# Low-rank adapter and paged attention on one core: another order of the first loads, of the first step's products, and of one weight read

## The chip, the cores and the metric

The kernel runs on one core of a Trainium2 chip. The metric is the device time of one execution in microseconds (us), the median of the runs shown. The core has a matrix engine (PE, with its weight load PEld), a vector engine (DVE), a scalar engine (ACT), GpSimd (POOL) and SyncE (SP), which here only issues DMAs. Each engine works through its own instructions in the order of the program. SP and ACT issue DMAs on hardware queues (q1 and q10 in the profile), POOL on a software queue (q0).

## The reference, cut to what matters

```
x: (8, 128, 512) f32
# 1. an adapter for each batch element
x = x + einsum('bsi,boi->bso', x, L0_weight[itok_B])          # L0_weight: (16, 512, 512)
# 2. paged attention, 32 query heads, 8 key heads, D = 128
q, k, v = x @ Wq.T, x @ Wk.T, x @ Wv.T
q, k = rope(rmsnorm(q) * wq_norm, pos), rope(rmsnorm(k) * wk_norm, pos)
                                                  # pos = seqlens[b] + 0..127
K = concat(k_cache[block_table[b]], k)            # 512 cached keys and 128 new ones
V = concat(v_cache[block_table[b]], v)            # cached keys from seqlens[b] on are masked
p = softmax(q @ K.T / sqrt(128) + mask)           # 4 query heads share a key head
out = x + (p @ V) @ Wo.T
```

All tensors are float32. The block table, the lengths and the adapter numbers are inputs that the kernel reads at run time.

## The kernel before, in words

**Steps.** The heads are cut into 4 groups `g` of 2 key heads and 8 query heads. A step is a pair (group, batch element): `i = 8 * g + b`, 32 steps in all. Step `i` computes the scores of its 8 query heads, one at a time (`h` = 0 to 7: a product on PE into `sc`, L977; the masked negative minimum on DVE, L987; the exponential on ACT, L1003; the normalisation on POOL, L1051; a transposition on DVE, L819). A place `8 * i + h` is called a slot.

**What PE does between the scores.** A list `main` holds the other products of a step in pieces of one fourth each: the projections of the next step (`project(i + 1, ...)`: `kv` for keys and values, `q0` and `q1` for four query heads each), the values product of the step before (`values`), its output product (`output`), and in the first group the adapter product (`lora_y`). The pieces are spread over the 8 heads by a share of the estimated cost (UNIT for a piece, TR for one 128x128 transposition). `turns_at` lists transpositions on PE at fixed heads: `turn_x`, `turn_x1` (x before and after the adapter), `turn_lora`, `turn_weights`, `turn_q`, `turn_k`.

**Products in flight.** Results of PE go to 4 PSUM tiles (`ps_mm`), shared by the transpositions and the products, and to 2 score tiles (`ps_sc`). What reads a product is not written down at once: `group` puts it into the list `pending`, and `run(pending)` writes it into the engines' queues later, once in each head after the scores, and at places of the prologue.

**After a projection.** `rotate` squares and sums the heads on ACT (L595), multiplies by the tables `CW` and `SW` on DVE (L607, L611) and adds the two on POOL (L620, L627); `norm_scales` makes the inverse root on POOL (L634, L635); its `rest` scales q on ACT (L640) and k on DVE (L643). `turn_q` and `turn_k` then transpose q and k on PE (L720, L711) and copy them out of PSUM (L721, L712); the scores of the step need them.

**The prologue** (L874 to L932) prepares step 0. It loads x of element 0, the adapter `raw_lora`, the rows of Wk and Wv (`raw_kv`) and of Wq (`raw_q`); transposes them on PE, with copies on ACT; computes the row numbers of the paged gathers from the block table `bt_i` (`row_numbers`: one cast on DVE at L334 and a chain of 14 small operations on POOL, L336 to L342; `row_tables` writes `key_ix` and `val_ix` on DVE, L348 and L349); computes the sine and cosine tables from `len_i` and `ivf` (`rope_angles` with 10 operations on DVE, then Sin and Abs on ACT; `rope_cos`; `rope_table` on DVE); gathers K and V of element 0 with indirect DMAs on POOL (L559); and makes the adapter products of the elements 0 and 1 (`lora_y`, added to `acc` on DVE at L533). The projection `q1` of step 0 is not in the prologue; it is the first in `main` of step 0.

**The order of the loads.** SP issues `raw_lora`, Wk, the 4 tiles of Wq for `q0`, x of element 1, the adapter 1, Wq for `q1`, x of element 2 and 8 tiles of Wo; ACT issues x of element 0, `len_i`, `ivf`, Wv, `ids_i` and `bt_i`; POOL issues the two norm weights (`wn`). `len_i`, `ivf`, `ids_i`, `bt_i` and `wn` are small and are broadcast to all 128 partitions. The plain loads of SP and ACT take their semaphores from one set of eight, so that an issue waits until the load that had the semaphore before has landed.

**Later weights.** From group 1 on the weights go through DRAM: `send_weights` writes them block-transposed, and `receive_weights` reads them back on ACT's queue (L473) at the slots of `reads_at`. The 8 tiles of Wo for group `g` are read at

```python
read_at(8 * (B * g + 1) + n - n // 4 * 2, key)
```

that is at heads 0 to 3 for the first half (`o0`, n = 0 to 3) and at heads 2 to 5 for the second (`o1`, n = 4 to 7) of the group's second step, whose output product needs them near its end.

Of the kernel before, what the change touches and what calls it, by code (L numbers as in the profile page):

```python
# [11 lines left out]
FP = mybir.dt.float32  # L12
I32 = mybir.dt.int32
# [5 lines left out]
P = 128  # L19
# [33 lines left out]
def lora_then_paged_attention(  # L53
# [50 lines left out]
    def load_x(b, eng=None):  # L104
        (eng or nc.sync).dma_start(out=acc[b], in_=x[b])

    load_x(0, nc.scalar)
    len_i = const.tile([P, B], I32, name="len_i")
    nc.scalar.dma_start(out=len_i, in_=seqlens.partition_broadcast(P))
    ivf = const.tile([P, H2], FP, name="ivf")  # L110
    nc.scalar.dma_start(out=ivf, in_=inv_freq.partition_broadcast(P))


    def weight_rows(kind, g, n, m=1):
# [22 lines left out]
    def load_first(kind, n, m, eng):  # L137
        eng.dma_start(
            out=first[kind][:, n * 512 : (n + m) * 512].rearrange("p (n i) -> p n i", n=m),
            in_=weight_rows(kind, 0, n, m).rearrange("(n p) i -> p n i", p=P),  # L140
        )
        for k in range(n, n + m):
            raw[kind, 0, k] = first[kind][:, k * 512 : (k + 1) * 512]
# [2 lines left out]

    lraw = {}

    def load_lora(b, dst):
# [8 lines left out]
        nc.sync.dma_start(  # L158
            out=dst.rearrange("p (j i) -> p j i", j=4),
            in_=lora_w[bass.ds(n, 1), :, :].rearrange("m (p j) i -> p (m j) i", j=4),  # L160
        )

    def lora_tile(b):
        t = lora.tile([P, 4, REP, QK], FP, tag="raw", name=f"lraw_{b}")
        return t.rearrange("p a r k -> p (a r k)")[:, 0 : 4 * HID]

    load_lora(0, first["lora"])
    load_first("kv", 0, 2, nc.sync)
    load_first("kv", 2, 2, nc.scalar)
    load_first("q0", 0, 4, nc.sync)  # L170
    load_x(1)
    load_lora(1, lora_tile(1))
    load_first("q1", 0, 4, nc.sync)
# [17 lines left out]
    ident = const.tile([P, P], FP, name="ident")  # L191
    make_identity(nc, ident)
    inner = const.tile([P, 1], FP, name="inner")
    quad = const.tile([P, 1], FP, name="quad")
    for a in range(4):
# [21 lines left out]
    for m in masks:  # L217
        nc.gpsimd.memset(m[:, :, LC, :], 0.0)

    nc.gpsimd.dma_start(out=wn[:, 1, :], in_=k_norm_w.partition_broadcast(P))  # L220
    nc.gpsimd.dma_start(out=wn[:, 0, :], in_=q_norm_w.partition_broadcast(P))
# [51 lines left out]
    def read_at(slot, key):  # L273
        reads_at.setdefault(slot, []).append(key)

    for g in range(1, G):
        before = 8 * B * (g - 1)
        for k, kind in enumerate(("kv", "q0", "q1")):
            for n in range(4):
                turn_when[before + 9 + 5 * (4 * k + n) // 2] = len(turns_of)  # L280
                turns_of.append((kind, g, n))
                read_at(before + 8 * (B - 2) + (2, 4, 6)[k] + n, (kind, g, n))
        for n, slot in enumerate((39, 42, 45, 62, 64, 66, 68, 70)):
            key = (f"o{n // 4}", g, n % 4)
# [155 lines left out]

    def turn_weights(key, copy=nc.scalar.copy):
        kind, a, n = key
        if n == 0:
            wT[kind] = wts.tile([P, 4, 4, 4, Q4], FP, tag=kind, name=f"w_{kind}_{a}")
        t = ps_mm.tile([P, HID], FP, tag="mm", name="wt_{}_{}_{}".format(*key))
        rows = raw.pop(key)
        for c in range(KC):
            nc.tensor.transpose(t[:, c * P : (c + 1) * P], rows[:, c * P : (c + 1) * P], ident)
        copy(
            wT[kind][:, n, :, :, :].rearrange("p b c j -> p c b j"),  # L450
            t.rearrange("p (c b j) -> p c b j", c=4, b=4),
        )
# [37 lines left out]


    def turn_x(b, copy=None):
# [2 lines left out]
    def turn_x1(b, copy=None):  # L495
        transposed(f"x1_{b}", chunks(acc[b]), [(x1T[b], 0, 4)], copy)
# [91 lines left out]
    def rotate(i, y, dst, ss, table, n, between=None):  # L588
# [285 lines left out]
    row_parts()  # L874
    table_set(AF.Sin)
    turn_x(0, on_act)
    for c in range(KC):
        turn_lora(0, c, on_act)
    for n in range(2):
        turn_weights(("kv", 0, n), on_act)  # L880
    row_numbers()
    rope_angles()
    row_tables((0,))
    for c in range(LC):
        gather_k(0, c)
    for c in range(LC):
        gather_v(0, c)
    rope_cos()
    for _, f in lora_y(0):
        f()  # L890
    for n in range(2, 4):
        turn_weights(("kv", 0, n), on_act)
    for n in range(4):
        turn_weights(("q0", 0, n), on_act)
    flush()
    turn_x1(0, on_vec)
    rope_table(1)
    rope_table(0)
    for n in range(2):
        turn_weights(("q1", 0, n), on_act)  # L900
    for what in ("kv", "q0"):
        for _, f in project(0, what):
            f()
        run(pending)
    for n in range(2, 4):
        turn_weights(("q1", 0, n), on_act)
    turn_x(1, on_act)
    for c in range(KC):
        turn_lora(1, c, on_act if c < 2 else on_vec, True)
    for j in range(GK):  # L910
        turn_kc(0, j, on_vec)
    run(pending)
    row_tables(range(1, G))
    nc.vector.scalar_tensor_tensor(
        out=lora_ix,
# [3 lines left out]
        op0=ALU.mult,  # L919
        op1=ALU.add,  # L920
    )
    for c in range(LC):
        gather_k(1, c)
    gather_lora(2)
    for _, f in lora_y(1):
        f()
    for _ in range(3):
        load_next()
    turn_q(0, 0, on_act)
    turn_k(0, 0, on_act)  # L930
    run(pending)
    make_mask(0)  # L932

# [2 lines left out]
    for i, (g, b) in enumerate(steps):  # L936
        s = st[i]
        main = []
        if i == 0:
            main += project(0, "q1")  # L940
        early = i >= B - 2
        if i and not early:
            main += values(i - 1, 0)
# [182 lines left out]
```

## Time and profile before

| | |
|---|---|
| median of 3 runs | 1208.49 us (1206.54 to 1209.66) |
| profiled execution, device time | 1210.85 us |
| its span, first to last instruction | 1209.1 us |
| PE busy | 1180.3 us (98%) |
| DVE, ACT, POOL busy | 729.9, 531.0, 675.2 us |
| DMA, mean over the span | 271 GB/s, 328.26 MB |
| first scores of step 0 and of step 1 start | 43.56 and 83.13 us |

The profile is of one execution. Times in it count from the first instruction. A row of the timeline gives start, duration, engine, line, operation and tiles, the count, and in brackets the idle time of the engine before it with what ended it. "ACTq", "SPq" and "POOLq" are the engines' sequencers, which issue DMAs and wait. "PEclk" is the share of full clock that PE was granted. The profiled execution lies 2.4 us above the median of the runs.

### The profile page before, as it was taken

How to read it: one execution, taken by the hardware profiler on the slowest of the kernel's cores; microseconds unless marked ns; L12 is line 12 of the kernel's file. 1: busy time of each engine (PE TensorE's matmuls, PEld its weight loads, DVE VectorE, ACT ScalarE, POOL GpSimd, SP SyncE). 2: the span in 40 equal slices, each digit the busy share in tenths (PEclk: the TensorE clock that was granted, in tenths of full speed). 3: DMA queues.
4: the chain of work that ended last, by engine and by line, in shares of the span. 5: the costliest groups of instructions: out<-in, count | busy, mean ns of one | idle time of the engine just before them, and what ended most of it. 6: DMA issues, size and time to landing. Idle time of an engine off the chain costs nothing.

```text
span 1209.1 us, 12947 instructions
## 1 busy us (share of the span) xinstructions
PE 1180.3 (98%) x3408; PEld 577.2 (48%) x3408; DVE 729.9 (60%) x1670; ACT 531.0 (44%) x1649; POOL 675.2 (56%) x778
## 2 busy tenths in 40 slices
PE   5989999999999999999999999999999999999998
PEld 3545544454444444444444444444444444444445
DVE  4456566556567666666656766666557655565651
ACT  4454444444444444444444444444444444444432
POOL 5464556455665556566555555655565556555540
PEclk9989999999999999999999999999999999999999
DMA  8267797887998989888898998888899897777761
GB/s 302 89 222 246 260 306 275 275 276 236 304 293 289 331 287 309 285 297 284 286 299 299 304 346 284 289 294 280 279 313 298 278 312 240 257 246 245 260 223 60
DMA packets 187496, 328.26 MB, mean 271 GB/s; under 512 B 13440, under 2 KB 106496, under 8 KB 178336
## 3 DMA queue, kind: packets, MB, share of 16 engines
q1 hardware_dynamic: 124112, 239.23, 59.1%
q10 hardware_dynamic: 50096, 48.22, 12.3%
q0 software_dynamic: 13216, 39.99, 9.8%
q8 instruction: 27, 0.44, 0.2%
q14 instruction: 45, 0.37, 0.1%
HBM read 195.27 MB, written 132.12 MB: 271 GB/s over the span
## 4 chain that ended last, share of the span: by engine, by line
PE 93%; DMA 2%; ACT 1%; POOL 1%; DVE 1%; issue 1%; ACTq 0%; SPq 0%
PE sc L977 22%; PE o L508 22%; PE out L508 18%; PE pj_q L508 18%; PE pj_kv L508 9%; PE y L508 2%; PE lw L430 1%; DMA bt_i<-in_itok_Bx_dram 1%; DMA w_o<-xw_o 1%; PE x L430 1%; PE kt L711 1%; DMA pT<-xp 0%; DMA xp<-tp 0%; ACT sq L595 0%; DVE p L987 0%
## 5 line engine op out<-in xcount | busy, mean ns | idle before, releaser
L987 DVE CUSTOM_DVE_ANT_0 p<-sc,mask 128x640 f32<-128x640 f32 x256 | 210.9, 824 | 406.8 <-PE sc L977 406.7
L1003 ACT ACTIVATE p<-p,mn 128x640 f32<-128x640 f32 x256 | 211.6, 826 | 327.9 <-DVE mn L987 322.8
L977 PE MATMUL sc<-kT,qT 128*128 128x512 f32 (+1 forms) x1024 | 320.2, 435 | 3.8 <-ACT qT L721 2.0
L1051 POOL TENSOR_SCALAR p<-p,rc 128x640 f32<-128x640 f32 x252 | 201.5, 800 | 195.8 <-DVE rc L1044 193.9
L977 PEld LDWEIGHTS sc<-kT,qT 128*128 128x128 f32 x1024 | 190.7, 191 | 230.2 <-issue 207.7
L508 PE MATMUL out<-w_o,oT 128*128 128x512 f32 (+1 forms) x528 | 235.1, 580 | 4.1 <-ACT p L1003 2.0
L508 PE MATMUL pj_q<-w_q,x1T 128*128 128x512 f32 x512 | 238.1, 595 | 0.5 <-issue 0.5
L508 PE MATMUL o<-pT,vc 128*128 128x512 f32 x512 | 237.2, 593 | 0.2 <-DMA pT<-xp 0.2
L819 DVE STREAM_TRANSPOSE tp<-p 128x640 f32<-128x640 f32 x252 | 210.9, 837 | 4.4 <-POOL p L1051 4.1
L559 POOL DMA_INDIRECT kc<-in_L_cond_k_cache_dram,key_ix x128 | 130.9, 1022 | 31.8 <-issue 30.2
L559 POOL DMA_INDIRECT vc<-in_L_cond_v_cache_dram,val_ix x128 | 128.2, 1002 | 31.2 <-issue 31.0
L640 ACT ACTIVATE q<-q,rs 128x128 f32<-128x128 f32 x256 | 81.9, 390 | 139.8 <-POOL q L627 132.8
L508 PEld LDWEIGHTS out<-w_o,oT 128*128 128x128 f32 x528 | 95.8, 190 | 97.0 <-issue 91.3
L508 PEld LDWEIGHTS pj_q<-w_q,x1T 128*128 128x128 f32 x512 | 92.9, 192 | 92.7 <-issue 91.0
L508 PEld LDWEIGHTS o<-pT,vc 128*128 128x128 f32 x512 | 92.2, 191 | 88.9 <-issue 81.3
L508 PE MATMUL pj_kv<-w_kv,x1T 128*128 128x512 f32 x256 | 116.7, 594 | 0.7 <-ACT x1T L432 0.7
L620 POOL TENSOR_TENSOR k<-sw 128x256 f32<-128x256 f32 x31 | 22.9, 739 | 158.8 <-PE kt L711 133.4
L627 POOL TENSOR_TENSOR q<-q,sw 128x512 f32<-128x512 f32 x61 | 77.2, 1266 | 47.8 <-DVE sw L611 47.7
L595 ACT ACTIVATE sq<-pj_q 128x128 f32<-128x128 f32 x256 | 70.6, 276 | 49.9 <-PE pj_q L508 41.2
L635 POOL TENSOR_TENSOR rs<-ss,mhalf 128x6 f32<-128x6 f32 x64 | 77.6, 1213 | 5.3
L508 PEld LDWEIGHTS pj_kv<-w_kv,x1T 128*128 128x128 f32 x256 | 46.0, 191 | 46.1 <-issue 44.5
L508 PE MATMUL o<-pT,vn 128*128 128x512 f32 x128 | 65.4, 593 | 0.0
(112 smaller groups left out, 865.8 us busy)
## 6 DMA issues: line engine op xcount, KB each, us to landing
xp<-tp SPq DMA_DIRECT2D x63, 1280.0 KB, 5.8
pT<-xp SPq DMA_DIRECT2D x63, 1280.0 KB, 7.0
xk<-tk SPq DMA_DIRECT2D x31, 512.0 KB, 7.5
kT<-xk SPq DMA_DIRECT2D x62, 256.0 KB, 6.4
xq<-tq SPq DMA_DIRECT2D x59, 256.0 KB, 4.4
qT<-xq SPq DMA_DIRECT2D x59, 256.0 KB, 5.3
st_q<-in_L_cond_Wq_dram ACTq DMA_DIRECT2D x24, 256.0 KB, 5.4
xw_q<-tw_q ACTq DMA_DIRECT2D x24, 256.0 KB, 4.3
```

What stands on the lines that cost most here:

```text
L430: nc.tensor.transpose(t[:, j, :], blk, ident)
L508: nc.tensor.matmul(y[0], lhsT=lhsT, rhs=rhs, start=(k == 0), stop=(k == len(pieces) - 1))
L559: nc.gpsimd.indirect_dma_start(out=dst[:, c, :], out_offset=None, in_=src, in_offset=bass.IndirectOffsetOnAxis(ap=rows[:, g, at : at + 1], ...
L595: nc.scalar.activation(sq, t[:, h, :], AF.Square, scale=float(D) ** -0.5, accum_out=ss[:, h : h + 1])
L627: nc.gpsimd.tensor_tensor(dst, cw, sw[:, 0:heads, :], ALU.add)
L635: nc.gpsimd.tensor_tensor(rs[:, 0:width], ss[:, 0:width], mhalf[:, 0:width], ALU.pow)
L640: nc.scalar.activation(q, q, AF.Identity, scale=rs[:, h : h + 1])
L819: nc.vector.transpose(u.tp[:, :, r, :], u.p.pop(r).rearrange("q (a k) -> q a k", a=4))
L977: nc.tensor.matmul(sc[:, lo:hi], lhsT=s.qT[j][:, r, :, :].rearrange("d h q -> d (h q)"), rhs=s.kT[j].rearrange("d a c i -> d (a c i)")[:, ...
L987: nc.vector.tensor_tensor_reduce(out=p, in0=sc[:, 0:LA], in1=masks[i % 2].rearrange("p a c i -> p (a c i)"), scale=1.0, scalar=3.0e38, op0 ...
L1003: nc.scalar.activation(p, p, AF.Exp, bias=unit.mn[:, one], scale=-1.0, accum_out=unit.sm[:, one])
L1051: nc.gpsimd.tensor_scalar(q, p, unit.rc[:, one], 1.0, ALU.mult, ALU.mult)
```

## The change

Seven things change.

1. `len_i`, `ivf` and `bt_i` are issued from POOL's queue, with the two `wn` loads, directly behind the identity matrix and ahead of POOL's other constants. `ids_i` stays on ACT, but is issued behind the copies of Wk.
2. The first adapter is loaded in two halves, and transposed by rows (`turn_lora_row`), its copies taking turns on ACT and DVE. Wv is issued and transposed ahead of it; one of its copies is on DVE.
3. `q1`'s rows of Wq are loaded in two halves, ahead of x and adapter of element 1.
4. In the prologue `rope_angles` comes behind `row_tables` and K's gathers, no longer ahead of them. V's gathers move from there to behind the projection of q0.
5. The projection `q1` of step 0 moves from step 0 into the prologue. The adapter product of element 1 moves the other way, into step 0, with `turn_x1(1)` and the four transpositions of Wo's first half behind it in `main`. `turn_q(0, 1)` moves from head 3 to head 2.
6. In step 0 the sum in `rotate` for q is made on DVE instead of POOL.
7. The second half of Wo (`o1`) is read one slot earlier in each later group.

The diff, cut to its core:

```diff
     load_x(0, nc.scalar)
-    len_i = const.tile([P, B], I32, name="len_i")
-    nc.scalar.dma_start(out=len_i, in_=seqlens.partition_broadcast(P))
-    ivf = const.tile([P, H2], FP, name="ivf")
-    nc.scalar.dma_start(out=ivf, in_=inv_freq.partition_broadcast(P))
...
-    load_lora(0, first["lora"])
+    load_first("kv", 2, 2, nc.scalar)
+    load_lora(0, first["lora"], 2)
     load_first("kv", 0, 2, nc.sync)
-    load_first("kv", 2, 2, nc.scalar)
     load_first("q0", 0, 4, nc.sync)
+    for n in (0, 2):
+        load_first("q1", n, 2, nc.sync)
     load_x(1)
     load_lora(1, lora_tile(1))
-    load_first("q1", 0, 4, nc.sync)
     load_x(2)
...
-    nc.scalar.dma_start(out=ids_i, in_=adapter_ids.partition_broadcast(P))
+    ident = const.tile([P, P], FP, name="ident")
+    make_identity(nc, ident)
...
-    nc.scalar.dma_start(
+    nc.gpsimd.dma_start(
         out=bt_i.rearrange("p c q -> p (c q)"),
         in_=block_table.rearrange("b n -> (b n)").partition_broadcast(P),
     )
+    len_i = const.tile([P, B], I32, name="len_i")
+    nc.gpsimd.dma_start(out=len_i, in_=seqlens.partition_broadcast(P))
+    ivf = const.tile([P, H2], FP, name="ivf")
+    nc.gpsimd.dma_start(out=ivf, in_=inv_freq.partition_broadcast(P))
     wn = const.tile([P, 2, D], FP, name="wn")
+    nc.gpsimd.dma_start(out=wn[:, 1, :], in_=k_norm_w.partition_broadcast(P))
+    nc.gpsimd.dma_start(out=wn[:, 0, :], in_=q_norm_w.partition_broadcast(P))
...
         if i == 0:
-            at(i, 1, True, lambda: turn_x1(1))
-            at(i, 3, False, lambda: turn_q(0, 1))
+            at(i, 2, False, lambda: turn_q(0, 1))
             at(i, 7, False, lambda: turn_q(1, 0))
-            for n, h in enumerate((5, 6, 6, 7)):
-                at(i, h, False, lambda n=n: turn_weights(("o0", 0, n)))
...
-            read_at(8 * (B * g + 1) + n - n // 4 * 2, key)
+            read_at(8 * (B * g + 1) + n - n // 4 * 3, key)
...
+    def turn_lora_row(b, j, copy):
+        if j == 0:
+            wT["lora"] = lora.tile([P, KC, 4, P], FP, tag="wT", name=f"wT_{b}")
+        rows = lraw[b].rearrange("p (j i) -> p j i", j=4)
+        transposed(f"lw_{b}_{j}", chunks(rows[:, j, :]), [(wT["lora"][:, :, j, :], 0, 4)], copy)
...
-            nc.gpsimd.tensor_tensor(dst, cw, sw[:, 0:heads, :], ALU.add)
+            add = nc.gpsimd if i or table else nc.vector
+            add.tensor_tensor(dst, cw, sw[:, 0:heads, :], ALU.add)
```

The prologue after the change, from its first transposition on:

```python
    turn_x(0, on_act)
    turn_weights(("kv", 0, 2), on_act)
    turn_weights(("kv", 0, 3), on_vec)
    for j in range(4):
        turn_lora_row(0, j, (on_act, on_vec)[j % 2])
    for n in range(2):
        turn_weights(("kv", 0, n), on_act)
    nc.scalar.dma_start(out=ids_i, in_=adapter_ids.partition_broadcast(P))
    row_numbers()
    row_tables((0,))
    for c in range(LC):
        gather_k(0, c)
    rope_angles()
    for _, f in lora_y(0):
        f()
    for n in range(2):
        turn_weights(("q0", 0, n), on_act)
    flush()
    rope_cos()
    for n in range(2, 4):
        turn_weights(("q0", 0, n), on_act)
    turn_x1(0, on_vec)
    for n in range(2):
        turn_weights(("q1", 0, n), on_act)
    rope_table(1)
    for _, f in project(0, "kv"):
        f()
    rope_table(0)
    run(pending)
    for _, f in project(0, "q0"):
        f()
    run(pending)
    for j in range(GK):
        turn_kc(0, j, on_vec)
    for n in range(2, 4):
        turn_weights(("q1", 0, n), on_act)
    run(pending)
    for c in range(LC):
        gather_v(0, c)
    for _, f in project(0, "q1"):
        f()
    turn_x(1, on_vec)
    for c in range(KC):
        turn_lora(1, c, on_vec if c % 2 else on_act, True)
    turn_q(0, 0, on_act)
    turn_k(0, 0, on_act)
    for c in range(LC):
        gather_k(1, c)
    row_tables(range(1, G))
    ...
    gather_lora(2)
    for _ in range(3):
        load_next()
    run(pending)
    make_mask(0)
```

And `main` of step 0, which began with `project(0, "q1")`:

```python
            main += lora_y(1)

            def second(n):
                run(pending)
                if n == 2:
                    turn_x1(1)
                turn_weights(("o0", 0, n))

            main += [(4 * TR * (1 + n // 2), lambda n=n: second(n)) for n in range(3)]
            main += [(4 * TR, lambda: turn_weights(("o0", 0, 3)))]
```

More of the change, by code (lines that the diff above doesn't have):

```diff
@@ L147, in lora_then_paged_attention, with load_lora @@
     lraw = {}
-    def load_lora(b, dst):
+    def load_lora(b, dst, parts=1):
         n = nc.values_load(
@@ L157, in load_lora @@
         lraw[b] = dst
[L158 to L161, printed above, removed]
+        for k in range(parts):
+            js = slice(4 * k // parts, 4 * (k + 1) // parts)
+            nc.sync.dma_start(
+                out=dst.rearrange("p (j i) -> p j i", j=4)[:, js, :],
+                in_=lora_w[bass.ds(n, 1), :, :].rearrange("m (p j) i -> p (m j) i", j=4)[:, js, :],
+            )
     def lora_tile(b):
@@ L187, in lora_then_paged_attention @@
     )
+    len_i = const.tile([P, B], I32, name="len_i")
+    nc.gpsimd.dma_start(out=len_i, in_=seqlens.partition_broadcast(P))
+    ivf = const.tile([P, H2], FP, name="ivf")
+    nc.gpsimd.dma_start(out=ivf, in_=inv_freq.partition_broadcast(P))
     wn = const.tile([P, 2, D], FP, name="wn")
+    nc.gpsimd.dma_start(out=wn[:, 1, :], in_=k_norm_w.partition_broadcast(P))
+    nc.gpsimd.dma_start(out=wn[:, 0, :], in_=q_norm_w.partition_broadcast(P))
     par = const.tile([P, 1], I32, name="par")
     nc.gpsimd.iota(par, pattern=[[0, 1]], base=0, channel_multiplier=1)
-    ident = const.tile([P, P], FP, name="ident")
-    make_identity(nc, ident)
     inner = const.tile([P, 1], FP, name="inner")
@@ L218, in lora_then_paged_attention @@
         nc.gpsimd.memset(m[:, :, LC, :], 0.0)
-    nc.gpsimd.dma_start(out=wn[:, 1, :], in_=k_norm_w.partition_broadcast(P))
-    nc.gpsimd.dma_start(out=wn[:, 0, :], in_=q_norm_w.partition_broadcast(P))
     lora_ix = const.tile([P, B], I32, name="lora_ix")
@@ L442, in turn_weights @@
         kind, a, n = key
-        if n == 0:
+        if kind not in wT:
             wT[kind] = wts.tile([P, 4, 4, 4, Q4], FP, tag=kind, name=f"w_{kind}_{a}")
@@ L876, in lora_then_paged_attention @@
     turn_x(0, on_act)
-    for c in range(KC):
-        turn_lora(0, c, on_act)
+    turn_weights(("kv", 0, 2), on_act)
+    turn_weights(("kv", 0, 3), on_vec)
+    for j in range(4):
+        turn_lora_row(0, j, (on_act, on_vec)[j % 2])
     for n in range(2):
         turn_weights(("kv", 0, n), on_act)
+    nc.scalar.dma_start(out=ids_i, in_=adapter_ids.partition_broadcast(P))
     row_numbers()
-    rope_angles()
     row_tables((0,))
@@ L885, in lora_then_paged_attention @@
         gather_k(0, c)
+    rope_angles()
+    for _, f in lora_y(0):
+        f()
+    for n in range(2):
+        turn_weights(("q0", 0, n), on_act)
+    flush()
+    rope_cos()
+    for n in range(2, 4):
+        turn_weights(("q0", 0, n), on_act)
+    turn_x1(0, on_vec)
+    for n in range(2):
+        turn_weights(("q1", 0, n), on_act)
+    rope_table(1)
+    for _, f in project(0, "kv"):
+        f()
+    rope_table(0)
+    run(pending)
+    for _, f in project(0, "q0"):
+        f()
+    run(pending)
+    for j in range(GK):
+        turn_kc(0, j, on_vec)
+    for n in range(2, 4):
+        turn_weights(("q1", 0, n), on_act)
+    run(pending)
     for c in range(LC):
         gather_v(0, c)
-    rope_cos()
-    for _, f in lora_y(0):
-        f()
[L891 to L907, printed above, removed]
-    for c in range(KC):
[L909 to L912, printed above, removed]
+    for _, f in project(0, "q1"):
+        f()
+    turn_x(1, on_vec)
+    for c in range(KC):
+        turn_lora(1, c, on_vec if c % 2 else on_act, True)
+    turn_q(0, 0, on_act)
+    turn_k(0, 0, on_act)
+    for c in range(LC):
+        gather_k(1, c)
     row_tables(range(1, G))
@@ L921, in lora_then_paged_attention @@
     )
-    for c in range(LC):
-        gather_k(1, c)
     gather_lora(2)
-    for _, f in lora_y(1):
-        f()
     for _ in range(3):
         load_next()
-    turn_q(0, 0, on_act)
-    turn_k(0, 0, on_act)
     run(pending)
@@ L939, in lora_then_paged_attention @@
         if i == 0:
-            main += project(0, "q1")
+            main += lora_y(1)
+            def second(n):
+                run(pending)
+                if n == 2:
[3 more added lines that the diff above has]
+            main += [(4 * TR, lambda: turn_weights(("o0", 0, 3)))]
         early = i >= B - 2
```

## The prediction

> **What bounds the kernel now.** I read the page first (engines and slices), then PE's waits, then windows of the prologue and step 0, then the timelines of PE, DVE, POOL, ACT and SP up to 90 us.
>
> ```profile
> PE 1180.3 (98%) x3408; PEld 577.2 (48%) x3408; DVE 729.9 (60%) x1670; ACT 531.0 (44%) x1649; POOL 675.2 (56%) x778
> PE   5989999999999999999999999999999999999998
> ```
>
> PE is the bound: busy 98%, and below nine tenths only in the first and third slices of 30 us. The change neither adds nor removes a product. So it can only gain or lose where PE waits, and where PE runs at half clock. PE's waits, longest first:
>
> ```profile
> PE lw L430 <- DMA raw_lora<-in_L_cond_weight_dram: 7.4, 1, 7.4
> PE x L430 <- DMA acc<-in_x_dram: 3.6, 1, 3.6
> PE kt L711 <- ACT qT L721: 2.2, 1, 2.2
> PE sc L977 <- ACT qT L721: 2.0, 1, 2.0
> PE out L508 <- ACT p L1003: 2.0, 1, 2.0
> PE sc L977 <- ACT kT L712: 1.8, 2, 0.9
> PE lw L430 <- ACT wT L432: 1.5, 1, 1.5
> PE out L508 <- DMA w_o<-xw_o: 1.3, 1, 1.3
> PE wt_q L448 <- ACT w_kv L449: 1.0, 1, 1.0
> PE wt_q L448 <- DVE acc L533: 0.7, 1, 0.7
> ```
>
> Up to 83.13 us (first scores of step 1) PE waits 20.3 us. Two waits lie later and are of one kind. The one named ACT p is at 428.97 us; p had long been done, but the last `w_o` read landed at 428.88. The other, at 707.62, names the DMA itself.
>
> Windows of 3.4 us (columns: busy PE, PEld, DVE, ACT, POOL; clock; DMA):
>
> ```profile
> 59.30:62.70 3.40, 1.40 (x9) 0.79 (x8) 2.51 (x8) 2.00 (x5) 1.51 (x2) 1.00 0.00 0
> 62.70:66.10 3.40, 3.40 (x7) 1.66 (x6) 2.67 (x7) 0.92 (x2) 0.80 (x1) 0.51 0.39 153
> 79.80:83.20 3.40, 0.40 (x2) 0.21 (x2) 1.48 (x3) 3.28 (x9) 2.70 (x4) 1.00 0.29 39
> 83.20:86.60 3.40, 3.40 (x9) 2.32 (x10) 1.00 (x3) 0.14 (x1) 2.50 (x3) 0.51 0.90 358
> ```
>
> A window in which PE was busy 1.4 us or less of 3.4 is followed by one at half clock, which loses 1.7 us. So a wait of 2 us costs 3.7.
>
> **The change part by part.** I walked the engines' queues in the new order, each instruction with its duration in the trace of before, and with 4 PSUM tiles. The old order walked in this way gives 43.6 us for the first scores (trace 43.56) and 83.2 for step 1 (83.13).
>
> *The loads.*
>
> ```profile
> 3.00:5.00 2.00, 1.09 (x4) 0.72 (x4) 0.37 (x3) 1.10 (x1) 1.70 (x6) 1.00 0.06 11
> 7.00:9.00 2.00, 0.00 (x0) 0.00 (x0) 0.00 (x0) 0.00 (x0) 0.00 (x0) 1.00 1.06 432
> raw_lora<-in_L_cond_weight_dram SPq DMA_DIRECT2D x1, 1024.0 KB, 9.5
> ivf<-in_inv_freq_dram ACTq DMA_DIRECT2D x1, 32.0 KB, 5.9
> ```
>
> From 3 to 5 us the DMA engines moved 11 GB/s, though Wv (issued 2.13) and the adapter (2.65) were queued; `ivf`, 32 KB issued ahead of both, landed only at 7.5. Row: the small loads hold up the large ones, on SP's queue too. The Trainium skill speaks against the change here: "DMA: Bandwidth & Descriptors", section "Issuing engines are not separate DMA queues", says that loads of all engines interleave on the same 16 DMA engines, and that issuing from several engines saves only issue time. By that rule the adapter lands at 12.1 as before. I go by the row. With the small loads gone, Wv follows x at about 3 us; at 0.38 MB/us (the windows after 7 us: 340 to 432 GB/s) and some 0.5 us to land, Wv is there at 5.3, the adapter's halves at 6.7 and 8.1, Wk 9.5, q0 12, q1 14.6. PE then transposes Wv and the adapter from 5.3 at the unwarmed 0.21 us each, and ends at 10.2 (before 15.3): a lead of 5 us. By the rule the lead is nothing and the walk ends 4.0 us later than by the row.
>
> *POOL's queue.* Five DMAs (0.74 us, then 0.57 each) stand ahead of POOL's constants: `inner` is ready at 5.5 (before 2.3), POOL's last constant at 7.0 (4.7). ACT's table instruction waits for that one, so the copy of x goes from 5.3 to 7.2; PE doesn't wait, since it has four PSUM tiles. `wn` took 7.8 us on this queue, so `bt_i`, issued at 1.4, lands at 9.2. DVE reaches it at 10.9, so I cost it at nothing. Each us after 10.9 would cost one.
>
> *DVE's order.* This takes the lead back. `row_tables` now stands ahead of `rope_angles`, so DVE waits for POOL's whole chain. The chain took 7.0 us (13.24 to 20.25) beside busy DVE; the same operation took half as long where DVE ran out of work (L337: 0.80, 0.68, then 0.41), so I take 5.5, and 7.0 as the other bound (+1.9). From 10.9: cast and chain to 16.7, angles (13.07 to 17.87 before, 4.8) to 21.6, then the sum into `acc`, which holds a PSUM tile. PE has finished what it can at 15.8 and waits 6.8 us for that sum. Then ACT's Sin, Abs, two copies, Sin, table load, two copies (5.3 us, by their rows) let the projection `kv` start at 26.4; before it was 25.94.
>
> *Behind it.* Two copies of K^T on DVE are behind `rotate`, and the last transposition of q1 needs the tile that `rotate` frees: 1.6 us of waits ahead of the q1 projection. That projection (3.4) takes the place of the adapter product (3.4). The copies of the second adapter on ACT and DVE by turns leave 0.2 of 1.48. V's gathers (4 x 1.25 on POOL) are behind `norm_scales` of q0 and have no reader before step 1: nothing; without that cover, 5. `ids_i` blocks ACT until the load eight places ahead has landed. I take a Wo tile, about 20; ACT's next is Sin at 21.6: nothing. Scores start between 43.7 and 45.0 (before 43.56).
>
> *Step 0.* q1 is projected early, so the wait for its qT at 62 us (2.0, and 1.7 of half clock) goes. The rotation of step 1's q1 is written one head later, so ACT no longer waits for POOL in head 7, and the tile that `kt` waited for is free: 2.25 and 1.7 of half clock go, the last 0.9 for kT stays. New: at the end of the prologue ACT squares q1 only after qT, kT and three DMA issues; POOL's norm is behind 9 gathers; DVE then has the sum (0.6, on POOL 1.27), mask, first and second `p`, and a transposition ahead of the adapter's sum. `turn_x1(1)` waits for that sum behind ACT's two exponentials: 3.3 us.
>
> *Wo.* The last read of `o1` is issued a head (3.7 to 4.5 us) earlier; missing were 1.97 and 1.27. Both go. The third group landed 1.0 us early anyway, and `o0` keeps 1 us or more. -3.2, bounds 0 and -3.3.
>
> The sum, in us:
>
> | | gone | new |
> |---|---|---|
> | waits | 7.4 adapter, 1.7 tiles at 22 and 23, 1.3 copies, 2.0, 2.25 | 0.6 Wv, 6.8 sum, 1.6 q1, 3.3 `turn_x1(1)` |
> | half clock | 1.3 adapter, 1.7, 1.7 | 2.2 Wv and adapter, 1.6 after the 6.8, 0.8 after the 3.3 |
> | Wo | 3.2 | |
>
> Gone 22.6, new 16.9: -5.7. Against the profiled execution, 1210.85, that is 1205.1; it lies 2.4 above the median, and from the median, 1208.5, it is 1202.8. The size of the half-clock terms depends on where the clock's windows fall. The skill's "TensorE: Matmul & The Clock Gate" (section "Part 1: The HAM clock gate") says that the window runs free of the program; the trace shows its length only. Moving it through the walk changes the sum by 2 either way.
>
> **The rivals.**
>
> *The loads keep their time* (the rule above: the change doesn't do what it says there). The prologue loses 4.0 of its gain: 1206.8, no measurable change. For it: all queues do share the engines. Against it: 11 GB/s with 3 MB issued.
>
> *ids_i blocks ACT* (slower). An issue waits for the landing of an earlier load:
>
> ```profile
> 3.90 1.26 SPq L138 DMA_DIRECT2D raw_q<-in_L_cond_Wq_dram  x1
> 12.14 0.34 SPq L105 DMA_DIRECT2D acc<-in_x_dram  x1
> ```
>
> SP stood from 5.2 until the adapter landed (12.12). If `ids_i` waits for the last Wo tile (landed at 30.5 before) rather than the first, Sin, both tables and all copies of Wq stand behind it. From 21.6 on each us costs one or a little more: at 30.5 the walk ends 10 us later, at 1212.8. Against it: the loads come earlier now, and eight places ahead is the first tile of Wo.
>
> *DVE doesn't hold the lead* (faster): if the angles run beside POOL's chain after all, `kv` starts near 22 and the time is 1198. Against it: DVE's rows of before follow the program's order.
>
> **How the numbers follow.** Forecast 0.58, loads as before 0.24, `ids_i` 0.09, lead kept 0.09. What a measurement can tell from no change is about 0.3%, 3.6 us: faster is under 1204.9, slower over 1212.1. The forecast's own range is 1199 to 1207 (clock 2, chain 1.9, loads 1.5, Wo). A fifth of it lies over 1204.9, and a fifth of the loads' rival under it: faster 0.60, same 0.30, slower 0.10. Leaving out a tenth at each end gives 1197.5 to 1210.
>
> **What would show it.** Right: the adapter's transpositions start by 7 us; DVE idle between L334 and L348 for some 5 us and the angles behind it; PE waiting 5 to 7 us for `acc` L533 in `wt_q`; no wait at scores 4 and 8 of over 1 us; a wait of 2 to 4 us for `turn_x1(1)`; no wait for `w_o`. Wrong: DMA under 50 GB/s after 4 us, ACT idle at `ids_i` past 22 us, or `bt_i` landing after 11.

## The result

The changed kernel takes 1211.23 us (median of 20 executions, 1208.25 to 1213.93), the kernel before 1209.67 us (20, 1206.54 to 1213.42). The ratio is 1.0010, 95% interval 1.0002 to 1.0018: 1.2 us slower, where 5.7 us less was forecast, and outside the range.

Its profiled execution took 1208.25 us, with a span of 1206.5; it is the fastest of the twenty. The page of it, PE's busy row and slices, answers to the first lines shown of before:

```profile
PE 1180.7 (98%) x3408; PEld 578.5 (48%) x3408; DVE 734.2 (61%) x1676; ACT 530.0 (44%) x1645; POOL 672.8 (56%) x779
PE   5799999999999999999999999999999999999998
```

PE does the same work, and only the first two slices are below nine tenths. PE's waits, longest first (total, times, longest):

```profile
PE wt_q L449 <- DVE acc L541: 5.2, 1, 5.2
PE lw L431 <- DMA raw_lora<-in_L_cond_weight_dram: 4.0, 1, 4.0
PE x L431 <- DMA acc<-in_x_dram: 3.7, 1, 3.7
PE x L431 <- DVE rc L1067: 3.6, 1, 3.6
PE sc L1000 <- ACT kT L721: 1.7, 2, 0.9
```

The wait for the adapter fell from 7.4 to 4.0 us only. The 5.2 us for the first sum into `acc` are new, as forecast, and so are the 3.6 us of `turn_x1(1)` (the fourth line: it names `rc`, but DVE's sum into `acc` ran just ahead of that, from 58.53 to 59.56, and PE went on at 59.71). The waits for `w_o` are gone, and those at scores 4 and ahead of `kt`. The first scores of step 0 start at 48.89 us (before 43.56, forecast 43.7 to 45.0), those of step 1 at 85.62 (before 83.13).

Next come three windows of the prologue (length; busy PE, PEld, DVE, ACT, POOL; clock; DMA share; GB/s), and four rows of the loads (KB, median us from issue to landing):

```profile
3.00:5.00 2.00, 1.16 (x5) 0.79 (x6) 0.00 (x0) 0.00 (x0) 1.90 (x9) 1.00 0.87 290
5.00:7.00 2.00, 1.90 (x8) 1.50 (x8) 1.09 (x10) 0.56 (x2) 1.29 (x9) 1.00 0.95 108
7.00:9.00 2.00, 0.00 (x0) 0.00 (x0) 0.63 (x1) 0.61 (x2) 0.00 (x0) 1.00 0.85 238
...
raw_lora<-in_L_cond_weight_dram SPq DMA_DIRECT2D x2, 512.0 KB, 8.6
bt_i<-in_itok_Bx_dram POOLq DMA_DIRECT2D x1, 64.0 KB, 4.9
wn<-in_L_cond_k_norm_w_dram POOLq DMA_DIRECT2D x1, 64.0 KB, 9.2
ivf<-in_inv_freq_dram POOLq DMA_DIRECT2D x1, 32.0 KB, 7.3
```

The slow stretch of before (11 GB/s from 3 to 5 us) has not gone, it has moved: from 5 to 7 us the DMA engines are busy 0.95 of the time and move only 108 GB/s. The halves of the adapter landed at 10.85 and 12.17, not at 6.7 and 8.1.

The clock, in windows of 3.41 us, laid so that the changes of the granted clock fall on their borders:

```profile
20.27:23.68 3.41, 1.20 (x11) 0.96 (x9) 2.78 (x8) 0.00 (x0) 2.44 (x5) 1.00 1.05 382
23.68:27.09 3.41, 0.46 (x2) 0.46 (x3) 3.12 (x5) 1.48 (x3) 1.95 (x2) 0.50 1.01 360
27.09:30.50 3.41, 3.41 (x17) 2.89 (x16) 1.99 (x5) 3.38 (x7) 0.00 (x0) 0.50 0.28 103
54.40:57.81 3.41, 1.66 (x10) 0.94 (x8) 1.04 (x6) 2.45 (x8) 0.80 (x1) 1.00 0.54 226
57.81:61.22 3.41, 1.51 (x13) 1.54 (x14) 1.82 (x3) 2.51 (x6) 0.80 (x1) 1.00 0.00 0
```

The wait of 5.2 us leaves two windows in a row with PE busy 1.20 and 0.46 us. Behind each of them comes a window at half clock, so that the second is itself at half clock. The wait of 3.6 us (56.07 to 59.71) is cut in two by the boundary at 57.81: 1.66 and 1.51 us of PE on either side, and no half clock follows. In another execution the boundary lies elsewhere. So I count, for every execution, the loss to the clock: (1 - mean granted clock) x span; the clock is given to three decimals, so one execution's loss is good to 0.6 us. What is left of the mean time, when all of this loss is taken off, is called the rest. The row of before is of the executions beside e1 to e4; each ratio is to executions of before on the same chip.

| kernel | median us | ratio to before, interval | clock loss, mean | rest |
|---|---|---|---|---|
| before | 1209.42 (42) | | 3.0 | 1206.4 |
| changed | 1211.23 (20) | 1.0010 (1.0002 to 1.0018) | 6.65 | 1204.3 |
| e1 before, Wo read alone | 1206.92 (14) | 0.9978 (0.9970 to 0.9986) | 2.4 | 1204.5 |
| e2 angles first | 1207.10 (14) | 0.9974 (0.9965 to 0.9984) | 3.5 | 1203.1 |
| e3 small loads behind | 1206.33 (16) | 0.9973 (0.9963 to 0.9982) | 3.4 | 1203.2 |
| e4 swap undone | 1213.19 (11) | 1.0027 (1.0017 to 1.0037) | 6.4 | 1206.4 |
| e5 sum first | 1208.65 (13) | 0.9994 (0.9985 to 1.0004) | 5.6 | 1203.2 |
| e6 second sum earlier | 1207.14 (21) | 0.9985 (0.9979 to 0.9992) | 2.8 | 1204.4 |
| e7 both waits filled | 1209.12 (13) | 1.0004 (0.9995 to 1.0012) | 1.0 | 1208.4 |
| e13 later wait filled | 1209.04 (13) | 1.0000 (0.9991 to 1.0008) | 4.0 | 1205.0 |
| e14 first wait filled | 1211.20 (13) | 1.0011 (1.0001 to 1.0021) | 3.8 | 1207.0 |
| e10 both prologue edits | 1203.04 (5) | 0.9945 (0.9932 to 0.9959) | 1.4 | 1201.2 |
| e8 e10 and e6 together | 1199.86 (5) | 0.9929 (0.9915 to 0.9942) | 0.2 | 1199.8 |
| e11 sum ahead of all | 1205.08 (6) | 0.9969 (0.9957 to 0.9981) | 5.6 | 1199.6 |

In brackets behind a median is the number of executions.

Not all of this loss is time, so the rest is a bound from below. The loss counts half clock also while PE only waits: of the two windows at half clock above PE was busy 0.46 and 3.41 us, so 1.9 of their 3.4 us of loss fell on work and 1.5 into the wait. The executions say the same. Over the 282 of these runs, each set against its own mean, an execution with 1 us more of loss took 0.41 us more (standard error 0.05; the changed kernel's twenty alone 0.26, error 0.16). Why it is no more is shown in part only. I use 0.41 below as the rate at which loss turns into time, with that doubt. And the rest still holds the slow start of the prologue, where the profile shows the full clock:

```profile
10.89 3.87 PE L431 MATMUL lw<-ident,raw_lora 128*128 128x128 f32 x16 [3.99 <-DMA raw_lora<-in_L_cond_weight_dram]
20.00 1.47 PE L449 MATMUL wt_q<-ident,raw_q 128*128 128x128 f32 x12
```

A transposition takes 0.24 us in the first row and 0.12 in the second.

The first two rows of the table are the answer in short: the mean time of their executions rose by 1.6 us (1210.97 against 1209.41), and the loss by 3.7. If all of that loss were time, the rest would have fallen by 2.1; at 0.41 the clock took some 1.5 (an estimate), and the rest hardly moved.

Below, differences between two kernels are differences of their ratios, times 1209 us. By the two intervals such a difference is good to some 1.5 us (an estimate).

### The profile page after: what moved, and what is told of

It reads as the page before. It is cut to its first block, busy times and chain, and to the rows that moved or that the text cites. A ratio compares the mean times of both kernels' runs of the same rounds, so it can differ in the third digit from the quotient of the medians.

```text
span 1206.5 us, 12952 instructions
## 1 busy us (share of the span) xinstructions
PE 1180.7 (98%) x3408; PEld 578.5 (48%) x3408; DVE 734.2 (61%) x1676; ACT 530.0 (44%) x1645; POOL 672.8 (56%) x779
## 3 DMA queue, kind: packets, MB, share of 16 engines
q0 software_dynamic: 13312, 40.10, 10.2%
## 4 chain that ended last, share of the span: by engine, by line
PE 95%; DMA 2%; POOL 1%; DVE 1%; ACT 1%; issue 0%; SPq 0%; ACTq 0%
PE o L516 23%; PE sc L1000 22%; PE pj_q L516 18%; PE out L516 18%; PE pj_kv L516 9%; PE y L516 2%; DMA w_q<-xw_q 1%; PE lw L431 1%; DMA raw_lora<-in_L_cond_weight_dram 1%; PE kt L720 1%; PE x L431 1%; POOL kc L567 0%; PE wt_q L449 0%; PE wt_o L449 0%; DVE acc L541 0%
## 5 line engine op out<-in xcount | busy, mean ns | idle before, releaser
L636 POOL TENSOR_TENSOR q<-q,sw 128x512 f32<-128x512 f32 x59 | 74.7, 1265 | 46.4 <-DVE sw L619 46.4
```

The costliest lines, as they stand in the source:

```text
L636: add.tensor_tensor(dst, cw, sw[:, 0:heads, :], ALU.add)
```

## The experiments

**The parts of the change.** Theory: the small loads hold the shared DMA engines from whichever queue; DVE's new order costs the 5.2 us; long waits cost clock beside their length; the swap in step 0 and the Wo read gain what was forecast. The rivals name the swap or chance.

*e1*, on the kernel before:

```diff
-            read_at(8 * (B * g + 1) + n - n // 4 * 2, key)
+            read_at(8 * (B * g + 1) + n - n // 4 * 3, key)
```

> The kernel before with one edit: the reads of the second half of Wo (o1) are issued a head earlier, as in the change. If the 3.2 us of the Wo step are real in every execution, this alone gives -3.2 us (-0.27%) against before, and no PE wait on w_o is left. Rival: the two waits are chance of the profiled execution, or come back elsewhere; then the time is within 1 us of before. By the Wo step alone, the rest of the change is then a loss of 4 to 5 us.

-2.7 us (interval -3.6 to -1.7), and no wait for `w_o` in its trace. The Wo step is real. What else was changed is then a loss of 3.9 us.

*e4*, on the changed kernel: `project(0, "q1")` heads step 0 again, `lora_y(1)` is in the prologue, and the transpositions are at their old heads.

```diff
-            at(i, 2, False, lambda: turn_q(0, 1))
+            at(i, 1, True, lambda: turn_x1(1))
+            at(i, 3, False, lambda: turn_q(0, 1))
...
-            main += lora_y(1)
+            main += project(0, "q1")
```

> The changed kernel with the swap undone: q1 of step 0 is again projected inside step 0, the second adapter product is in the prologue, turn_x1(1), turn_q(0,1) and the Wo turns are at their old places. Theory by the prediction's sum: the swap gains the waits of 2.0 and 2.25 us with their half clock and costs a 3.3 us wait, so undoing it costs 2 to 4 us (1213 to 1215). Rival: the 3.6 us wait of turn_x1(1) and the later first scores make the swap the loss, and undoing it gains 2 to 4 us (1207 to 1209).

2.1 us slower than the changed kernel, and two of PE's waits came back (2.0 and 2.2 us in the kernel before):

```profile
PE kt L723 <- ACT w_o L453: 2.6, 1, 2.6
PE sc L994 <- ACT qT L733: 2.0, 1, 2.0
```

The swap gains 2.1 us. e4 is the kernel before with the Wo read and the new prologue; against e1 it is 5.9 us slower. So the whole loss is in the prologue.

*e2*, the angles back ahead of `row_tables`:

```diff
     row_numbers()
+    rope_angles()
     row_tables((0,))
     for c in range(LC):
         gather_k(0, c)
-    rope_angles()
```

> The changed kernel with the angles put back ahead of row_tables and of the K gathers, so that DVE computes them beside POOL's chain of row numbers. Theory: DVE's order costs the 5.2 us wait of wt_q for acc and the half clock of 23.7 to 30.5 us behind it; then that wait is under 1.5 us, kv projection starts 4 to 5 us earlier (about 26 us), and the time is 4 to 7 us under the changed kernel, about 1206. Rival: K's rows come later by the same 5 us, the scores wait for K instead, first scores stay at 48 to 49 us and the time within 1 us of the changed kernel.

4.4 us faster than the changed kernel. The wait for `acc` fell, but not under 1.5 us:

```profile
PE wt_q L449 <- DVE acc L541: 3.3, 1, 3.3
```

The projection `kv` started at 26.50. The loss fell by 3.1 us, the rest by 1.2. The first scores came at 47.82, close to what the rival said; its time was wrong.

*e3*, the five small loads on SP's queue behind the two halves:

```diff
     load_lora(0, first["lora"], 2)
+    (bt_i, len_i, ivf, wn, wn: the five dma_starts, on nc.sync)
     load_first("kv", 0, 2, nc.sync)
```

> The changed kernel with the small loads (block table, lengths, frequencies, norm weights) issued on SP's queue directly behind the two adapter halves instead of on GpSimd's queue. Theory (the small loads occupy the shared DMA engines from whichever queue): the adapter halves now land at 7 to 8.5 us instead of 10.85 and 12.17, PE's 4.0 us wait for raw_lora shrinks under 1 us, the small loads land at about 11 to 13, and block-table cast stays near 15 or comes earlier; the sum into acc then waits longer for DVE, so the time gains 0 to 3 us. Rival (the engines are simply not up to speed before 7 us, or SP's two issues are late): the halves land within 1 us of 10.85 and 12.17 as in the changed kernel.

4.5 us faster, more than expected; the rest fell by 1.1 us, the loss by 3.3. Windows and two timeline rows of its trace:

```profile
3.00:5.00 2.00, 1.32 (x5) 0.96 (x6) 0.32 (x3) 0.51 (x2) 0.29 (x3) 1.00 0.95 319
5.00:7.00 2.00, 1.73 (x8) 1.33 (x7) 0.23 (x1) 0.87 (x2) 0.00 (x0) 1.00 0.94 297
...
8.00:9.00 1.00, 1.00 (x7) 1.00 (x6) 0.00 (x0) 0.31 (x1) 0.00 (x0) 1.00 0.35 92
9.00:10.00 1.00, 1.00 (x7) 1.00 (x6) 0.46 (x1) 0.28 (x1) 0.00 (x0) 1.00 0.21 61
10.00:11.00 1.00, 1.00 (x6) 0.77 (x4) 0.23 (x1) 0.59 (x1) 0.00 (x0) 1.00 0.29 106
...
7.54 3.48 PE L431 MATMUL lw<-ident,raw_lora 128*128 128x128 f32 x16 [0.80 <-DMA raw_lora<-in_L_cond_weight_dram]
13.43 1.33 PE L449 MATMUL wt_kv<-ident,raw_kv 128*128 128x128 f32 x8 [2.42 <-DMA raw_kv<-in_L_cond_Wk_dram]
```

With nothing small ahead of it the adapter is there at 7.5, as the prediction had wanted it. The slow stretch is still there, at 8 to 11 us, and now Wk behind it is late (2.42 us). It did not come from a want of loads: SP had issued Wk at 6.43 and the first part of Wq at 7.51. So a slow stretch of two to three us stood where small loads stood: on ACT's queue (`len_i` and `ivf`, before), on GpSimd's (changed) and on SP's (here). What is left to choose is who is behind them.

**The clock.** *e6* writes the second sum earlier: the scaling of q1 waits until the first exponential is issued, and the sum is ahead of the transposition of `p`.

```diff
-            main += lora_y(1)
+            main += [(0.6, f) for _, f in lora_y(1)] + [(0.1, lambda: run(pending))]
...
             now[0] = 8 * i + h
-            run(pending)
+            if i or h:
+                run(pending)
```

> The changed kernel with the second adapter's sum written a few DVE instructions earlier in step 0 (its four products all in head 0, the sum behind the second p and ahead of the transposition of p, the scaling of q1 behind the first exponential). Theory: the 3.6 us wait of turn_x1(1) shrinks to about 1.5 us, and with it the cooling behind it in the runs where the clock's window fell badly: 2 to 4 us under the changed kernel, 1207 to 1209. Rival: that wait never cost clock (the profiled run shows none behind it) and the freed time is lost at the next wait: gain under 1 us.

3.0 us faster than the changed kernel. PE's waits in its trace:

```profile
PE wt_q L449 <- DVE acc L541: 6.0, 1, 6.0
...
PE x L431 <- DVE acc L541: 1.4, 1, 1.4
```

The wait fell from 3.6 to 1.4, and the loss from 6.65 to 2.8; the rest did not move (1204.4 against 1204.3), though a shorter wait should have lowered it. At 0.41 the loss that went is worth 1.6 us, which leaves 1.4 of the 3.0 for the wait (an estimate). In this trace the wait for the first sum is 0.8 longer than in the other.

*e9* and *e12* are the changed kernel twice more, for their traces.

> The changed kernel once more, for a second trace. Its profiled execution was the fastest of 20 and shows half clock only behind the wait of 5.2 us (mean loss of the 20 executions 6.6 us, of this trace 3.4). Theory: here the windows fall differently, and half clock also stands behind the 3.6 us wait of turn_x1(1) at about 60 us (one or two windows of 3.4 us); loss 5 to 7 us, time 1210 to 1213. Rival: the further loss comes from other places, spread over the span.

> The changed kernel a third time, with the same expectation: windows of half clock behind the waits of 5.2 and 3.6 us and nowhere else, loss 3.4 to 7 us; rival: elsewhere.

They took 1208.92 and 1209.83 us, with 3.4 us of loss in each trace, which for e9 is less than expected. e9 shows it behind the first wait alone; e12 shows one window behind each:

```profile
57.84:61.25 3.41, 0.85 (x8) 0.88 (x9) 2.27 (x5) 2.06 (x5) 1.38 (x2) 1.00 0.00 0
61.25:64.66 3.41, 3.41 (x12) 2.38 (x11) 0.07 (x1) 1.53 (x3) 0.00 (x0) 0.50 0.00 0
23.78:27.19 3.41, 0.00 (x0) 0.00 (x0) 3.29 (x5) 0.98 (x2) 2.14 (x3) 0.99 1.06 380
27.19:30.60 3.41, 3.38 (x15) 3.05 (x16) 1.80 (x4) 3.38 (x7) 0.00 (x0) 0.51 0.40 148
```

The same wait of 3.6 us, with the boundary at 57.84 and the start of the wait later, leaves PE 0.85 us of work, and half clock follows. Here both windows at half clock are full of work. Still, no trace shows more than 3.4 us, and the loss of the executions is 6.65 in the mean. Three kernels fill the waits with products that nobody reads, and leave what PE waits for alone:

```diff
     rope_cos()
+    keep_warm(5)      # e7: 5 products of 128x512, e14: 4, e13: none
     for n in range(2, 4):
         turn_weights(("q0", 0, n), on_act)
...
                 if n == 2:
+                    keep_warm(3)  # e7 and e13: 3, e14: none
                     turn_x1(1)
```

> The changed kernel with extra products whose results nobody reads: five of 128x512 where PE waits 5.2 us for acc, three where it waits 3.6 us for turn_x1(1); they add to the computation and take nothing from it, and the waits that DVE sets stay where they are. Theory (half of the lost time is clock, not waiting): PE stays busy through both, the half clock of 23.7 to 30.5 us goes, mean loss to the clock falls from 6.6 to 1.5 to 3.5 us, and the time falls by 3 to 5 us to 1206 to 1208 although PE does 7 us more work. Rival (the loss is the waits themselves or lies elsewhere): the time stays at 1211, or rises by what the extra products overhang.

> The changed kernel with three extra products of 128x512, read by nobody, in the 3.6 us wait of turn_x1(1) alone. Theory: about half of the changed kernel's mean clock loss of 6.6 us stands behind this wait, though its three traces show it once; the loss falls to 3 to 4 us and the time to 1207 to 1209, while the wait itself keeps its end. Rival: the clock loss is behind the wait of 5.2 us alone; loss and time stay at 6 to 7 and 1211.

> The changed kernel with four extra products of 128x512, read by nobody, in the 5.2 us wait of wt_q for acc alone. Theory: the two windows of half clock behind it (3.4 us) go in most executions; the loss falls from 6.6 to 3 to 4 us and the time by 1 to 3 us, to 1208 to 1210. Rival: the loss is behind the later wait alone and stays at 6 to 7; the time stays at 1211 or rises.

With both filled the loss falls from 6.65 to 1.0 us, with the later one alone to 4.0, with the first alone to 3.8: 2.7 and 2.8 of it stand behind the two waits, about half each. The time hardly follows: e13 gains 1.2 us, e7 0.7 and e14 nothing, and with an uncertainty of 1.5 none of these is clear of zero. e7 and e14 fall short of what was expected. At 0.41 the loss that went would be worth 1.1 us (e13), 1.2 (e14) and 2.3 (e7). In the traces of e14 and e7 kv starts at 30.39 and 32.65 us, no earlier than the 30.29 of the changed kernel; waits of 2.5 (e14) and of 1.7 and 1.6 us (e7) are left behind the extra products, with 6.8 us of half clock, and e7's execution had Wv late by 1.6 us. So the waits are shown to bring the half clock; that the half clock brings the lost time is not shown by these three.

**A better version.** *e10* has the small loads on SP behind the adapter and Wk, and the angles first. *e8* has e6's edit as well.

```diff
     load_first("kv", 0, 2, nc.sync)
+    (bt_i, len_i, ivf, wn, wn: the five dma_starts, on nc.sync)
     load_first("q0", 0, 4, nc.sync)
...
     row_numbers()
+    rope_angles()
     row_tables((0,))
```

> The changed kernel with three edits together: the small loads on SP's queue behind the adapter and Wk, the angles ahead of row_tables, and the earlier second sum of the run x1_early. Theory: adapter halves land at 7 to 8.5 us, Wk at 9.5 to 10.5, kv projection starts at 22 to 24 us, first scores at 40 to 43, no PE wait over 2 us between 12 and 83 us, and the time is 1200 to 1204. Rival: the edits share one gain (as the two runs before each gave the same 4 us), Wq or the K rows become the next bound, and the time is 1206 to 1207, no better than either alone.

> The run of the three edits without the earlier second sum: small loads on SP's queue behind Wk, angles ahead of row_tables, step 0 as in the changed kernel. Theory: it loses again the 3.6 us wait of turn_x1(1) less 1.4, and the cooling behind it: 1202 to 1205, that is the prologue is worth 6 to 9 us against the changed kernel and step 0 the rest. Rival: the prologue alone gives nearly all, 1200 to 1201.

e10 is 7.9 us under the changed kernel and e8 9.8: 0.9929 of the kernel before, faster than both. PE's rows of e8:

```profile
7.98 3.68 PE L431 MATMUL lw<-ident,raw_lora 128*128 128x128 f32 x16 [0.97 <-DMA raw_lora<-in_L_cond_weight_dram]
...
18.00 1.50 PE L449 MATMUL wt_q<-ident,raw_q 128*128 128x128 f32 x12 [1.45 <-DMA raw_q<-in_L_cond_Wq_dram]
20.68 0.66 PE L449 MATMUL wt_q<-ident,raw_q 128*128 128x128 f32 x4 [1.18 <-DVE acc L541]
...
42.36 1.35 PE L1000 MATMUL sc<-kT,qT 128*128 128x512 f32 x4 [0.84 <-ACT kT L721]
...
50.91 0.66 PE L431 MATMUL x<-ident,acc 128*128 128x128 f32 x4 [1.38 <-DVE acc L541]
```

After the adapter no wait is longer than 1.5 us, the trace has no half clock from the first product to the last, and the first scores stand at 42.36.

*e5* and *e11* try the other order: the sum into `acc` ahead of the angles (e5, on the changed kernel), and that with the small loads behind the first part of Wq and the row numbers behind the sum too (e11, on e8).

```diff
     row_numbers()
+    (lora_y(0), the copies of q0, flush(), turn_x1(0, on_act))
+    rope_angles()
     row_tables((0,))
     for c in range(LC):
         gather_k(0, c)
-    rope_angles()
```

> The changed kernel with the adapter's sum into acc written ahead of the angles and of row_tables (x1T copied by ACT, the cosines behind it). The small loads stay on GpSimd's queue. Theory: the 5.2 us wait of wt_q for acc was made by DVE's order; with it gone kv projection starts at 22 to 25 us instead of 30.3, no window of half clock stands there (mean loss to the clock 2 to 4 us instead of 6.6), and the time is 4 to 7 us under the changed kernel, 1204 to 1207. Rival: angles and K's rows come 5 us later in exchange and the wait only moves to kct or to rotate; first scores stay at 48 to 49 us and the time stays within 1.5 us of the changed kernel.

> The run of the three edits with the small loads behind the first half of Wq instead of ahead of it, and with the first sum into acc ahead of row numbers and angles. Theory: Wq lands about 2 to 4 us earlier, the waits of 1.5 (Wq) and 1.2 us (acc) go, kv projection starts at 19 to 21 us; K's rows then come 2 to 3 us late and take some of it back: 1197 to 1200. Rival: K's rows and the tables become the bound of the prologue by more than was gained: 1200 to 1203.

Both fell short: e5 gains 1.9 us on the changed kernel and e11 is 4.8 slower than e8. The wait for the first sum is gone in both, and the gathered rows of K are late instead (`kct` is their transposition). PE's waits, e5 and then e11:

```profile
PE kct L711 <- DMA kc<-in_L_cond_k_cache_dram,key_ix: 2.7, 3, 1.0
```

```profile
PE kct L711 <- DMA kc<-in_L_cond_k_cache_dram,key_ix: 4.9, 2, 4.1
```

And the clock behind e11's:

```profile
27.00:30.00 3.00, 0.00 (x0) 0.00 (x0) 2.97 (x7) 2.83 (x15) 2.39 (x3) 0.99 1.00 384
30.00:40.00 10.00, 7.03 (x19) 4.22 (x20) 5.04 (x13) 2.48 (x8) 7.84 (x9) 0.50 0.25 81
```

e8 and e11 have the same rest (1199.8 and 1199.6), and differ in the loss, 0.2 against 5.6. That is not 5.4 us of clock: in the last window PE waited for 3.0 of the 10 us at half clock, so 1.5 of its 5.0 us of loss fell into waits. At 0.41 the loss makes 2.2 of the 4.8 us (an estimate); how the other part divides among the waits isn't settled. What sets e11 apart is one wait of 4.1 us where e8 has several of 1 us.

## Why the prediction was wrong, point by point

**What failed, by size.** Of its -5.7, the terms of granted half clock made -1.0 (1.7 and 1.7 gone, 1.6 and 0.8 new), all else -4.7 (the unwarmed transpositions among it, in which the profile shows the full clock). Measured are +3.7 for the granted half clock, and for all else something between -2.1, if every us of that loss is time, and about nothing, at 0.41. By parts: Wo -3.2 forecast, -2.7 measured; the swap -2.0 (gone 2.0, 2.25 and 3.4 of half clock; new 1.6, 3.3 and 0.8) and -2.1; the prologue's -0.5 (what is left of the sum) and +5.9. Two steps of it failed.

**The loads.** "I go by the row. With the small loads gone, Wv follows x": this is the step that failed first. The small loads were not gone, only on another queue. Wv did come, at 4.89 (5.3 forecast); the adapter's halves came at 10.85 and 12.17 (6.7 and 8.1 forecast), and its transpositions ended at 14.8 in place of 10.2. Of the lead of 5 us, 0.5 was there. The row of 11 GB/s was read rightly as small loads holding up large ones, and e3 shows that the adapter can be had at 7.5. What was not asked is what they do on the queue to which they are moved. The rule of the Trainium skill in "DMA: Bandwidth & Descriptors", section "Issuing engines are not separate DMA queues", that all queues share the same DMA engines, had been weighed and put aside; it fits what came: small loads on GpSimd's queue held up the adapter on SP's (first half at 10.85, against 7.5 in e3). The rival built on it (4.0 us) had the mechanism, and about the size: all else is 2.6 to 4.4 us above the forecast, by the two ways of counting the clock. Its time of 1206.8 leaves out that the half clock grew.

**The clock.** "1.6 after the 6.8, 0.8 after the 3.3": the loss behind the two waits is 2.8 and 2.7 us (e14, e13). The rule from before (busy 1.4 us or less of 3.4, then one window at half clock) held in every window of 3.41 us shown: 1.20, 0.85, 0.46 and 0.00 were followed by half clock, 1.51 and 1.66 were not. The count of windows was wrong. A wait of 5 to 7 us empties two windows, and was priced as one; a wait of 3.3, which can lie in one window or be cut in two, was priced at half of one window, and brought more than one and a half in the mean. The price of a window, 1.7 us, was too high where PE waits in it: for the first wait the 1.9 us of loss that fell on work in the profiled execution are near the 1.6 forecast. So the loss was mis-sized by 4.7 (-1.0 forecast, +3.7 measured); how much of that is time stays open, some 1.9 at 0.41 (an estimate).

**DVE's order.** Right by mechanism, and its pieces by size. The chain took 5.0 us (5.5 forecast), the angles 4.8. DVE's rows:

```profile
15.40 0.22 DVE L335 CAST pages<-bt_i 128x128 f32<-128x128 int32 x1
19.22 0.18 DVE L349 TENSOR_SCALAR key_ix<-pages 128x32 int32<-128x32 f32 x1 [3.60 <-POOL pages L340]
25.49 1.09 DVE L541 TENSOR_TENSOR acc<-y,acc 128x512 f32<-128x512 f32 x1
```

The cast was to be reached at 10.9, and stood at 15.40 because the copies of the late adapter are ahead of it. `bt_i` landed at 6.35, so its cost of nothing was right. With the 4.5 us of delay at the cast, kv started at 30.29 (26.4 forecast). The wait was 5.2 and not 6.8, since PE came to it 5.7 us late (21.5, forecast 15.8) and the sum only 4.0 (26.6, forecast 22.6). e2 shows what the order cost: 4.4 us.

**Step 0 and Wo.** Right: no wait for `w_o`, none over 1 us at scores 4 and ahead of `kt`, and 3.6 us for `turn_x1(1)` (3.3). That its release hangs on ACT fits e6, where the scaling of q1 is put behind the first exponential and the wait is 1.4; e6 moves the sum on DVE too, so the two are not told apart.

**The other rivals.** `ids_i` was issued at 16.51, before ACT's next work, and cost nothing. DVE did hold the lead back, so the faster rival fell; with the loads and the angles in the better order (e10) the time is 1203.0, where it had 1198.

## What to carry to other kernels

A small broadcast load can cost the transfers behind it from whatever queue it is issued: move it behind what is needed first, not to another queue. Long waits on PE bring half clock, by the number of windows that they can empty: waits of up to 1.5 us left a loss of 0.2 (e8), waits of 5.2 and 3.6 one of 6.65. But half clock costs only what PE does in it, so the mean granted clock bounds the loss of time and doesn't measure it; hold it against the times of single executions. A profiled execution is one draw of where the windows fall; the granted clocks of all executions say whether it was a typical one.

## What the runs showed of the hardware

- While five small loads, 228 KB in all, stood ahead of large ones, the DMA moved 61 to 108 GB/s for two to three us, with a busy share of 0.95 from GpSimd's queue and of 0.21 to 0.35 from SP's. Why the shares differ so was not tried.
- Half clock behind a wait can fall on the wait itself: PE was busy 0.46 us of one window of 3.41 at half clock. Over 282 executions, 1 us of loss by the mean granted clock went with 0.41 us of time.
- The three profiled executions of the changed kernel have a loss of 3.4 us each, the twenty timed ones, the first of these three among them, 6.65 in the mean. Whether profiling itself moves the phase was not tried.
